# A two-layer graph network on one core: which engine turns the last 256 columns of the attention matrix, the order of the last products, the room of one tile, and four planned delays

## The chip, the core and the metric

The kernel runs on one core of a Trainium2 chip. The core has a matrix engine (TensorE, PE in the profile, with its weight loads as PEld), VectorE (DVE), ScalarE (ACT), GpSimd (POOL) and SyncE (SP), whose queue issues nearly all transfers between on-chip memory and DRAM. Each engine takes its instructions in a fixed order. The metric is the device time of one execution in microseconds. A difference of about 0.2% (some 4 us here) is what a measurement of this kernel can tell from no change.

## The reference

There are 3327 nodes with 256 features, and a sparse weighted adjacency matrix `adj`. Layer 0 makes two steps (`STEPS = 2`); each has a dense attention and a product with the normalised adjacency matrix. Layer 1 is a graph attention with four heads, masked by `adj > 0`.

```python
# layer 0, from h = relu(layernorm(x)); two steps
logits = (Xa @ W1.T @ W2.T) @ (Xa @ W3.T).T        # 3327 x 3327
probs  = softmax(logits)
A      = probs where the largest, up to a sum of 0.9, are kept, then rescaled by row
Xf, Xa = R @ Xf, A @ Xa                            # R = (adj + I) / its row sums
Z      = Z + Xf @ U1[n].T + Xa @ U2[n].T
# layer 1
e    = leaky_relu(s[:, i] + d[:, j]) where adj > 0, else -inf    # 4 heads
attn = softmax(e); out = elu(attn @ hp)            # per head, 64 columns of hp = h @ W
```

## The kernel before

Everything is fp32. The 3327 rows are padded to `NT = 26` tiles of 128 (`NP = 3328`). The program is not issued in the order of the source: each piece of work is handed to a planner (`Plan.put`) with an engine, an estimated length, a rank, the pieces it needs, the buffers it takes and gives back, and a delay `lag` after which its result is taken to be there. `Plan.order` runs through these estimates once while the program is built and writes each engine's fixed order from them. On the chip nothing of the estimates is left: an engine waits where a semaphore tells it to. A delay that is estimated too short therefore leaves the program right, but puts instructions in an order in which an engine stands and waits.

**Layer 0, one row tile of the attention.** A `Row` takes a tile `e` of 128 x 3328 (four buffers `e`, and every fifth row the room called `qq`). `logits` (L905) fills PSUM in four parts of 1024, 1024, 1024 and 255 columns; `exps` (L920) takes the exponential into `e`, with a row sum for each part, which `row_sum` adds. A search on ScalarE, GpSimd and VectorE finds a threshold for each part of a row, and `drop` (L1075, VectorE, four pieces) sets what lies below it to zero. Then the tile has to be transposed, because TensorE contracts over partitions. Of the 52 row tiles, 49 (`BLOCKED`: all 26 of step 1, 23 of step 2) go this way:

- The first 3072 columns: VectorE turns each stretch of 1024 columns in 32 x 32 blocks (`turn_blocks`, L1112), one transfer puts the stretch into DRAM (`put_blocks`, L1116, 512 KB), and four transfers bring it back with the blocks in their transposed places (`get_blocks`, L1121, 128 KB each in runs of 256 bytes). `exps` had stored the columns of these stretches with a stride of two, which makes these runs.
- The last 256 columns: TensorE turns them as two 128 x 128 products with the identity into PSUM (`turn`, L1087, tile `px`), ScalarE or VectorE copies them to `et` (L1098), and `attend` (L1105) uses them.

`attend_blocks` (L1128) multiplies the 24 returned column tiles with `rhs`; the two of `et` come in between, before the last eight. The remaining three rows of step 2 are turned on TensorE alone.

Beside it, `Full` (L1153) multiplies the adjacency matrix, loaded tile by tile (L1147), with `main` in step 1 and with `c` in step 2. These products have no hurry and stand in the order where the attention leaves TensorE free. After the attention of a row in step 1, `finish1` turns and projects it; its two results of 256 columns go to a PSUM tile `px` (two buffers for all users), ScalarE copies them to `ystage` (`stage`, L1347; two buffers), and a transfer stores them (L1358).

**Layer 1** works on four column blocks `b` of 832 nodes. For each of 26 source tiles `j`, VectorE computes the weights `e` of four heads (`exponents`, L1763, four instructions of 832 columns), TensorE multiplies them with `main` (`product`, L1779; the block is cut in two halves `c` of 416 columns) and sums them (`sums`, L1793). Two source tiles' products are followed by their two sums. Seven buffers hold `e`: four of the pool `e`, then half of the room of `c`, then both halves of the room of `rhs`. The last three may be taken once layer 0 has left the rooms. At the end of a block, `leave` copies the sums out of PSUM (L1842, L1848), and seven times TensorE turns 128 nodes (L1866), VectorE divides (L1904, L1905), ScalarE takes relu and exponential, GpSimd adds `x1` (L1918), VectorE joins (L1922) and a transfer stores. In the last block nothing follows that could hide this.

Of the kernel before, what the change touches and what calls it, by code (L numbers as in the profile page):

```python
# [587 lines left out]
def fast(  # L588
# [58 lines left out]
    with ExitStack() as l0:  # L647
# [23 lines left out]
        blocks = spill.tile([3, 4, P, 2 * P], F32, name="blocks")  # L671
# [194 lines left out]
        plan = Plan(dict(rows=1, mvs=3, pl=2, px=2, acca=1, accf=1, et=3, at=4, y=1, e2=3, mask=2, e5=1, qg=2, **BUFS))  # L866
# [4 lines left out]
        class Row:  # L871
# [3 lines left out]
                "b w t0 t1 t2 u g k2 p0 p1 p2 p3 D0 D1 D2 v z r0 s0 s1 s2 h x th tq mid dh kh fl d up h0 h1 room zs cnt "  # L875
# [38 lines left out]
            def exps(self, k):  # L914
                pl = self.pl.pop(k)
                to = self.e[:, PART * k : PART * k + pl.shape[1]]
                if k < 3 and self.i < BLOCKED[self.n]:
                    to = to.rearrange("p (g q t) -> p g t q", g=4, t=2)
                    pl = pl.rearrange("p (g t q) -> p g t q", g=4, t=2)
                S.activation(  # L920
                    to,
                    pl,
                    AF.Exp,
                    accum_out=(self.p0, self.p1, self.p2, self.p3)[k],
                )

            def row_sum(self):
                k = self.NAMES.index("p0")
                S.activation(self.sc[:, k + 4 : k + 8], self.sc[:, k : k + 4], AF.Copy, accum_out=self.s)
# [170 lines left out]
            def attend(self, g):  # L1100
# [3 lines left out]
                for j in range(4 * g, min(4 * g + 4, NT)):  # L1104
                    T.matmul(  # L1105
                        self.acc, et[:, j - 4 * g, :], rhs[self.n][:, j, :], start=(j == 0),
                        stop=j == NT - 1 and self.i >= BLOCKED[self.n],
                    )

            def turn_blocks(self, g):  # L1110
                part = self.e[:, g * PART : (g + 1) * PART].rearrange("p (g s t) -> p g t s", g=4, t=2)
                V.transpose(part, part)  # L1112

            def put_blocks(self, g):
                src = self.e[:, g * PART : (g + 1) * PART].rearrange("p (g w) -> p g w", g=4)
                nc.sync.dma_start(blocks[g].rearrange("g p w -> p g w"), src)  # L1116

            def get_blocks(self, g, o):
                part = slice(o * P // 4, (o + 1) * P // 4)
                src = blocks[g, :, :, o * P // 2 : (o + 1) * P // 2].rearrange("g (b s) w -> s (g b) w", b=4)  # L1120
                nc.sync.dma_start(self.e[part, g * PART : (g + 1) * PART].rearrange("p (c w) -> p c w", w=P // 2), src)  # L1121

            def attend_blocks(self, js, stop):
                for j in js:
# [3 lines left out]
                    T.matmul(self.acc, lhs, rhs[self.n][:, j, :], start=(j == 0), stop=stop and j == js[-1])  # L1128
# [180 lines left out]
        def finish1(row, done, rank):  # L1309
# [73 lines left out]
            y = plan.put("SP", 0.5, r + 0.3, store, needs=[a], give=["ystage"], lag=3.0)  # L1383
# [120 lines left out]
        def search(row, rank, keys, stats_of, fresh):  # L1504
# [4 lines left out]
            for g in range(2):  # L1509
# [8 lines left out]
                for k in (2 * g, 2 * g + 1):  # L1518
                    got.append(
                        plan.put("ACT", 1.15 if k < 3 else 0.5, rank - 2.5, row.exps, k, needs=[a], give=["pl"])  # L1520
# [32 lines left out]
            for o in range(4):  # L1553
                a = plan.put(
                    "DVE", 1.07 if o < 3 else 0.4, rank - 1.0, row.drop, o, needs=[a], hold=1.0 if o < 3 else 0.3,
                    lag=0.15 if o < 3 else 1.5,
# [4 lines left out]
        def attention(row, rank, total, drops, right):  # L1561
            a = None
            if row.i < BLOCKED[row.n]:
                come = []
                for g in range(3):
                    b = plan.put("DVE", 1.25, rank - 1.001, row.turn_blocks, g, needs=[drops[g]])
# [5 lines left out]
                last = plan.put("PE", 0.22, rank - 0.01, row.turn, 6, needs=[drops[3]], take=["px"])  # L1572
                last = plan.either(
                    ("ACT", 0.27, row.turned_by_s), ("DVE", 0.39, row.turned_by_v), rank - 2.6, 6, needs=[last],
                    take=["et"], give=["px"],
                )
                for j in (0, 4, 8, 12, 24, 16, 20):
                    if j == 24:
# [539 lines left out]
```

## Time and profile before

| what | value |
|---|---|
| time, median of 3 runs | 2105.58 us (2104.02 to 2105.99) |
| the profiled execution's own time | 2100.08 us |
| its span in the profile | 2098.2 us |
| granted TensorE clock, mean | 0.994 |
| DRAM read and written | 242.86 MB and 93.05 MB |

The profile's first part gives each engine's busy time; a busy TensorE includes matmuls whose ends overlap. In a timeline each line has start, length, engine, line, operation, output and inputs, shapes and count; a bracket at the end holds the idle time of that engine just before and what ended it. A table by windows has one row for a stretch, with the busy microseconds (and instruction counts) of PE, PEld, DVE, ACT and POOL, the granted TensorE clock, the busy share of the 16 DMA engines (overlapping packets can carry it over 1) and the GB/s moved.

### The profile page before, as it was taken

The page shows a single profiled execution, that of the slowest core. Times are in us where ns is not written, and L with a number is a line of the kernel's source. Part 1 is how long each engine was busy: PE and PEld are TensorE (multiplying, and loading weights), DVE is VectorE, ACT ScalarE, POOL GpSimd, SP SyncE. Part 2 cuts the span into 40 slices and gives each one's busy share as a digit, 9 for nine tenths or more (in the row PEclk, how much of TensorE's full clock was granted, in tenths as well). Part 3 has the DMA queues.
Part 4 walks back from the last instruction along what each step waited for, and adds up shares of the span by engine and source line. Part 5 has one row for each costly group of instructions (what it writes and reads, how often), then busy time and mean ns, then how long its engine had stood idle before and what let it go on. Part 6 is the DMA issues. An engine that isn't in the chain of part 4 may idle for free. (4 is left out here: it accounts for less than half of the span.)

```text
span 2098.2 us, 34334 instructions
## 1 busy us (share of the span) xinstructions
PE 2037.8 (97%) x10695; PEld 1415.2 (67%) x10695; DVE 1729.7 (82%) x4105; ACT 1300.0 (62%) x2480; POOL 990.7 (47%) x2170
## 2 busy tenths in 40 slices
PE   8999999999999989989999999999999999999997
PEld 6477777878787778767878787787877333333332
DVE  5689897778876871578998979988987999999895
ACT  5767665666556621777778776778652547465552
POOL 4476654446544630567778777777772000000001
PEclk9999999999999999999999999999999999999999
DMA  4188888678877685697787888887743544453341
GB/s 116 45 190 186 194 180 195 168 152 196 189 183 172 176 186 138 199 232 165 181 189 176 203 188 191 185 191 192 182 126 89 157 141 142 125 147 115 112 127 34
DMA packets 580513, 338.56 MB, mean 161 GB/s; under 512 B 327931, under 2 KB 533281, under 8 KB 580321
## 3 DMA queue, kind: packets, MB, share of 16 engines
q1 hardware_dynamic: 579424, 336.06, 66.4%
q8 instruction: 87, 1.43, 0.3%
q14 instruction: 106, 0.86, 0.1%
q10 hardware_dynamic: 896, 0.21, 0.0%
HBM read 242.86 MB, written 93.05 MB: 160 GB/s over the span
## 5 line engine op out<-in xcount | busy, mean ns | idle before, releaser
L959 ACT ACTIVATE junk<-e,sc 128x3327 fp8e5<-128x3327 f32 x147 | 451.0, 3068 | 31.4 <-POOL sc L996 29.8
L1128 PE MATMUL acca<-rhs,e 128*128 128x256 f32 x1872 | 426.8, 381 | 4.6 <-DMA e<-blocks 4.6
L1128 PEld LDWEIGHTS acca<-rhs,e 128*128 128x128 f32 x1872 | 364.9, 197 | 48.7 <-issue 6.0
L1153 PE MATMUL accf<-c,at 128*128 128x256 f32 x1352 | 316.5, 385 | 17.1 <-DMA at<-in_adjt_dram 8.5
L1153 PE MATMUL accf<-main,at 128*128 128x257 f32 x1352 | 313.3, 381 | 5.4 <-ACT main L1304 2.5
L1153 PEld LDWEIGHTS accf<-c,at 128*128 128x128 f32 x1352 | 252.8, 192 | 67.5 <-DMA at<-in_adjt_dram 10.2
L1153 PEld LDWEIGHTS accf<-main,at 128*128 128x128 f32 x1352 | 250.4, 190 | 54.3 <-issue 11.5
L1022 DVE MAX8 cands<-y 128x8 f32<-128x205 f32 (+1 forms) x832 | 242.9, 361 | 3.6
L1918 POOL TENSOR_TENSOR qq<-qq 128x256 f32<-128x256 f32 x4 | 3.0, 759 | 457.0 <-ACT qq L1914 457.0
L1017 DVE SCALAR_TENSOR_TENSOR y<-e,sc 128x1639 f32<-128x1639 f32 x84 | 165.1, 1965 | 62.9 <-POOL sc L1007 61.7
L920 ACT ACTIVATE e<-pl 128x1024 f32<-128x1024 f32 (+1 forms) x168 | 152.9, 920 | 75.4 <-PE pl L905 74.7
L1752 ACT ACTIVATE et<-at 128x448 bf16<-128x448 f32 (+1 forms) x204 | 112.6, 552 | 128.6 <-DVE e L1763 73.3
L1779 PE MATMUL pl<-e,main 128*64 128x416 f32 x1024 | 190.4, 517 | 0.1
L1075 DVE SCALAR_TENSOR_TENSOR e<-e,thr 128x1024 f32<-128x1024 f32 (+1 forms) x168 | 178.4, 1066 | 2.4 <-DMA at<-in_adjt_dram 0.3
L905 PE MATMUL pl<-kt,qg 64*128 64x512 f32 (+1 forms) x832 | 173.7, 536 | 0.4 <-ACT qq L920 0.4
L1112 DVE STREAM_TRANSPOSE e<-e 128x1024 f32<-128x1024 f32 x117 | 146.1, 1248 | 3.7
L1779 PEld LDWEIGHTS pl<-e,main 128*64 128x64 f32 x1024 | 70.3, 137 | 111.0 <-issue 91.5
L1763 DVE SCALAR_TENSOR_TENSOR e<-c,low,et 128x832 f32<-128x832 f32 x128 | 128.8, 1070 | 6.1 <-issue 3.2
L905 PEld LDWEIGHTS pl<-kt,qg 64*128 64x128 f32 x832 | 71.5, 186 | 83.4 <-issue 76.2
L1751 ACT ACTIVATE at<-at 128x448 f32<-128x448 f32 (+1 forms) x204 | 110.8, 543 | 25.7 <-DMA at<-in_adjt_dram 25.6
L1763 DVE SCALAR_TENSOR_TENSOR e<-qq,low,et 128x832 f32<-128x832 f32 x120 | 120.5, 1073 | 4.1 <-PE accf L1793 2.9
L959 ACT ACTIVATE junk<-qq,sc 128x3327 fp8e5<-128x3327 f32 x35 | 107.4, 3068 | 10.7 <-POOL sc L996 10.4
(550 smaller groups left out, 3540.7 us busy)
## 6 DMA issues: line engine op xcount, KB each, us to landing
at<-in_adjt_dram SPq DMA_DIRECT2D x414, 256.0 KB
blocks<-e SPq DMA_DIRECT2D x117, 512.0 KB
e<-blocks SPq DMA_DIRECT2D x468, 128.0 KB
at<-in_adjt_dram SPq DMA_DIRECT2D x102, 192.0 KB
blocks<-qq SPq DMA_DIRECT2D x30, 512.0 KB
qq<-blocks SPq DMA_DIRECT2D x120, 128.0 KB
at<-in_adjt_dram SPq DMA_DIRECT2D x52, 128.0 KB
ys<-ystage SPq DMA_DIRECT2D x26, 256.0 KB
```

Source lines behind the costliest of these rows:

```text
L905: T.matmul(pl[:, lo : lo + m], qg[self.n, self.i // 4][half, self.i % 4, :], kt[half, 512 * k : 512 * k + m], start=True, stop=True,)
L920: S.activation(to, pl, AF.Exp, accum_out=(self.p0, self.p1, self.p2, self.p3)[k],)
L959: S.activation(junk[:, :N], self.e[:, :N], fn, bias=t, scale=-1.0, accum_out=dst, saturate=False)
L1017: V.scalar_tensor_tensor(self.y[:, : hi - lo], self.e[:, lo:hi], self.up, self.e[:, lo:hi], ALU.is_lt, ALU.mult, accum_out=(self.h0, self. ...
L1022: V.max(self.cands[:, a * PIECES // 2 + k, :], self.y[:, at[k] - lo : at[k + 1] - lo])
L1075: V.scalar_tensor_tensor(piece, piece, self.thr[:, o : o + 1], piece, ALU.is_gt, ALU.mult)
L1112: V.transpose(part, part)
L1128: T.matmul(self.acc, lhs, rhs[self.n][:, j, :], start=(j == 0), stop=stop and j == js[-1])
L1153: T.matmul(self.acc[:, : self.w], self.at[j // JC][:, j % JC, :], self.src[:, j, : self.w], start=(j == 0), stop=(j == NT - 1),)
L1752: S.activation(to, src, AF.Sign)
L1763: V.scalar_tensor_tensor(held["e"][:, k, :], extra["both"][b % 2][:, k, :], low[:, j, k : k + 1], held["mask"], ALU.max, ALU.mult,)
L1779: T.matmul(q["acc"][a][k * FH : (k + 1) * FH, c, :C], main[:, j, h * FH : (h + 1) * FH], held["e"][:, h, c * C : (c + 1) * C], start=(j == 0),
```

## The change

- **Last 256 columns.** The third stretch of a blocked row is now 1280 columns. VectorE turns it in one instruction, which needs the third and fourth `drop`; it is put with one transfer of 640 KB and comes back with four of 160 KB. The two products with the identity, their copy and `attend` on `et` are gone for these rows. `exps` writes the last part with two instructions of 128 and 127 columns, each with its own sum.
- **Last products of layer 1.** In the last block, the last six source tiles are multiplied and summed for the first half of the columns, one tile after the other, then for the second half. The first half is copied out and its three turns stand between the products of the second.
- **Room of the first tile.** The tiles `j` with `j % 7 == 0`, so also `j = 0`, use half of the room of `c`; the four buffers of the pool follow.
- **Delays in the plan.** Store of `ystage`: 7.0 in place of 3.0; loads of the adjacency matrix: 4.0 in place of 3.3; after the fourth `drop`: 0.15 in place of 1.5.

In the built program TensorE has 98 products with the identity fewer (78 in place of 176 on the attention tiles); the number of products with `rhs` is the same. In the order that the planner writes, all products of `Full` in step 2 now stand ahead of the first product of layer 1; before, 26 of them stood between its first four matmuls and the rest.

```diff
@@ class Row
             def exps(self, k):
                 pl = self.pl.pop(k)
-                to = self.e[:, PART * k : PART * k + pl.shape[1]]
-                if k < 3 and self.i < BLOCKED[self.n]:
-                    to = to.rearrange("p (g q t) -> p g t q", g=4, t=2)
-                    pl = pl.rearrange("p (g t q) -> p g t q", g=4, t=2)
...
+                to = to.rearrange("p (g q t) -> p g t q", q=P, t=2)
+                if k < 3:
+                    S.activation(to, pl.rearrange("p (g t q) -> p g t q", g=4, t=2), AF.Exp, accum_out=sums[k])
+                else:
+                    S.activation(to[:, 0, 0, :], pl[:, :P], AF.Exp, accum_out=self.p3)
+                    S.activation(to[:, 0, 1, : m - P], pl[:, P:], AF.Exp, accum_out=self.p4)
...
+            def part(self, g):
+                return self.e[:, g * PART : (g + 1) * PART if g < 2 else NP]
+
             def turn_blocks(self, g):
-                part = self.e[:, g * PART : (g + 1) * PART].rearrange("p (g s t) -> p g t s", g=4, t=2)
+                part = self.part(g).rearrange("p (g s t) -> p g t s", s=P, t=2)
                 V.transpose(part, part)
@@ def finish1
-            y = plan.put("SP", 0.5, r + 0.3, store, needs=[a], give=["ystage"], lag=3.0)
+            y = plan.put("SP", 0.5, r + 0.3, store, needs=[a], give=["ystage"], lag=7.0)
@@ def search (drops)
-                    lag=0.15 if o < 3 else 1.5,
+                    lag=0.15,
@@ def attention
-                    b = plan.put("DVE", 1.25, rank - 1.001, row.turn_blocks, g, needs=[drops[g]])
+                    b = plan.put(
+                        "DVE", 1.25 if g < 2 else 1.55, rank - 1.001, row.turn_blocks, g, needs=drops[g : g + 1 + g // 2]
+                    )
...
-                last = plan.put("PE", 0.22, rank - 0.01, row.turn, 6, needs=[drops[3]], take=["px"])
-                last = plan.either(
-                    ("ACT", 0.27, row.turned_by_s), ("DVE", 0.39, row.turned_by_v), rank - 2.6, 6, needs=[last],
-                    take=["et"], give=["px"],
-                )
-                for j in (0, 4, 8, 12, 24, 16, 20):
-                    if j == 24:
-                        a = plan.put("PE", 0.864, rank, row.attend, 6, needs=[last, a], give=["et"])
-                        continue
+                for j in range(0, NT - 2, 4):
+                    js = range(j, j + 4 if j < 20 else NT)
                     a = plan.put(
-                        "PE", 1.728, rank, row.attend_blocks, range(j, j + 4), j == 20, needs=[come[j // 8], a, right],
+                        "PE", 0.432 * len(js), rank, row.attend_blocks, js, needs=[come[j // 8], a, right],
@@ def full
-                plan.put("SP", 0.4, rank, f.load, q, needs=[after], take=["at"], lag=3.3) for q in range(-(-NT // JC))
+                plan.put("SP", 0.4, rank, f.load, q, needs=[after], take=["at"], lag=4.0) for q in range(-(-NT // JC))
@@ def attend_neighbours
+            LATE = 6
...
-                                if k < 4
-                                else extra["e"][k - 4]
+                                if 0 < k < 5
+                                else extra["e"][max(k - 4, 0)]
...
+                    if b == 3 and j >= NT - LATE:
+                        for c in range(2):
+                            r = rank if c == 0 else r0 + 9.0
+                            p_ = plan.put("PE", 0.71, r, product, 0, (c,), needs=[x_, last_acc, halves[c]])
+                            p_ = plan.put("PE", 0.71, r, product, 1, (c,), needs=[x_, y_, p_])
+                            halves[c] = plan.put(
+                                "PE", 0.76, r, sums, (c,), needs=[p_, last_den], give=[mine] if c else []
+                            )
+                        continue
...
+                def leave_half(c, q=q):
+                    if c == 0:
+                        q["ot"] = scr.tile([P, 2 * W], F32, name="y").rearrange("p (k w) -> p k w", k=2)
+                        q["ot"] = [q["ot"][:, 0], q["ot"][:, 1], extra["den"]]
+                    for k in range(2):
+                        S.copy(q["ot"][k][:, c * C : (c + 1) * C], q["acc"][k][:, c, :C])
+                    S.copy(q["ot"][2][:, c * C : (c + 1) * C], q["den"][c][:, :C])
```

## The prediction

> **What bounds the kernel now.** I read the busy times first, then the table by windows, then TensorE's waits, then the timeline around the longest of them and at the end.
>
> ```profile
> PE 2037.8 (97%) x10695; PEld 1415.2 (67%) x10695; DVE 1729.7 (82%) x4105; ACT 1300.0 (62%) x2480; POOL 990.7 (47%) x2170
> ```
>
> ```profile
> 700.00:800.00 100.00, 92.07 (x416) 75.44 (x415) 72.14 (x197) 34.13 (x64) 37.87 (x83) 0.97 0.91 201
> ...
> 1100.00:1200.00 100.00, 98.28 (x466) 80.82 (x466) 91.63 (x264) 74.34 (x137) 79.94 (x173) 1.00 0.85 190
> ...
> 1700.00:1800.00 100.00, 100.00 (x735) 37.03 (x733) 98.39 (x115) 60.33 (x153) 0.00 (x0) 1.00 0.49 142
> ```
>
> TensorE is the bound nearly everywhere: 98 of 100 us in the attention, 100 in layer 1, with VectorE close behind (92 and 98). What it does not work it waits, and a share of that has names:
>
> ```profile
> PE accf L1153 <- DMA at<-in_adjt_dram: 10.5, 6, 6.2
> PE px L1087 <- ACT ystage L1347: 8.5, 3, 7.2
> PE accf L1153 <- ACT main L1164: 5.4, 5, 3.4
> PE acca L1128 <- DMA e<-blocks: 4.6, 6, 1.7
> ```
>
> ```profile
> 334.59 0.38 PE L1087 MATMUL px<-ident,e 128*128 128x128 f32 x2
> 334.81 1.90 PE L1153 MATMUL accf<-main,at 128*128 128x257 f32 x8
> ...
> 750.99 0.59 ACT L1347 COPY ystage<-px 128x512 f32<-128x512 f32 x1 [9.55 <-DMA ys<-ystage]
> 751.63 0.69 PE L1087 MATMUL px<-ident,e 128*128 128x128 f32 x2 [7.18 <-ACT ystage L1347]
> 752.11 3.25 PE L1128 MATMUL acca<-rhs,e 128*128 128x256 f32 x8
> ...
> 907.24 5.99 PE L1153 MATMUL accf<-c,at 128*128 128x256 f32 x16 [6.18 <-DMA at<-in_adjt_dram]
> ...
> 1164.49 1.97 PE L1128 MATMUL acca<-rhs,e 128*128 128x256 f32 x8 [1.72 <-DMA e<-blocks]
> ```
>
> The reader is to see three things. Two turns hold TensorE for 0.22 us (334.59 to 334.81). At 751 ScalarE waits for the store of an earlier `ystage`, keeps a tile `px`, and a turn waits for that. After such a gap the work is slow: eight matmuls take 3.25 us where they take 1.97 at 1164, sixteen take 5.99 where 3.62 is usual; the granted clock of that window is 0.97.
>
> **The change part by part.** The sum is made in the profiled execution's time, 2100.08 us; the median of the runs shown is 5.5 us above it.
>
> *The turns of 49 rows.* 98 products with the identity go: 49 x 0.22 = 10.8 us off the bounding engine. The products on `et` become products on `e` of the same 0.38 us. Hidden: the longer turn on VectorE, 1.248 x 1280/1024 = 1.56, so 49 x 0.31 = 15 us, against 20 copies of 0.42 that go; the extra exponential on ScalarE. One of 255 columns takes 0.385 and its read 0.20; the shortest ScalarE rows are 0.19, so one of 128 is near 0.29 and the pair adds 0.39, 19 us in all, against 29 copies of 0.37 that go. VectorE idles 8 us in 100 in the fullest attention window above, ScalarE 25; these cover it. Without the cover VectorE's net 7 us would lie on the path. Term -10.8.
>
> *The wait for `px`.* A blocked row took four tiles `px` and takes three; the turn that waited 7.18 us no longer exists, and a store planned at 7.0 lets the planner put ScalarE's copy later. The gap cost 7.18 and then 3.25 - 1.9 = 1.4 of slow work; two more such waits cost 1.3. What is late next is the projection of the next row, which takes the following `px`; the attention and `Full` stand between. Bounds: -9.9 (all gone) to 0 (another taker waits instead). I take -9.9, since the waiting instruction is removed.
>
> *The loads of the adjacency matrix.* At 907 the loads stand on SP's queue behind eight `get_blocks` issues that take 8.07 us from 894.11. In the new order two loads stand after each four. Gap plus slow work: 6.18 + 2.4 = 8.6. Bounds -8.6 to 0; half, -4.3, because these four-issue groups each carry more bytes.
>
> *The later third stretch.* It waits for a fourth `drop` (0.45) and 0.31 more of turning: 0.76 us. It moves 256 KB more per row, which at the 190 GB/s of the window is 1.35 us. And TensorE wants it sooner: without the two `et` products (0.87) before the last eight. Together 3.0 us of slack go in each row. From the trace's packet records, the last 256-byte packet of a third stretch ended a median of 5.8 us (step 1) and 4.2 us (step 2) before the matmul that needs it; where TensorE did stand waiting, this distance was 1.4 to 2.3, so about 1.5 of it is completion and cannot be used. Usable now 4.3 and 2.7; left 1.3 and -0.3. Each stall moves TensorE back against VectorE and gives the next rows slack, so I do not pay it 23 times. Bounds: 0, to 0.5 us in each of 49 rows, 25 us. I take 6, a little above the 4.6 that waits on `e<-blocks` cost now. Behind a waiting matmul stands everything on TensorE: the logits of later rows, `Full`, and with them ScalarE and VectorE. On SP the larger puts and gets are as many as before (147 and 588), and the loads behind a put now wait for the longer turn; the four loads ahead (`at`) cover 0.3 us.
>
> The Trainium skill speaks against this part twice. "VectorE: DVE Perf Modes", section "Rules for kernel authors", gives a 128 x 128 transpose to TensorE when PSUM may hold the result, because VectorE turns only blocks of 32 x 32. By that rule the part would be a loss: its gain of 10.8 would go and its cost of 6 would stay, a sum 10.8 higher. The page's ground is the path alone; here 0.22 us of the full engine is traded for time of engines with idle time. "DMA: Bandwidth & Descriptors", section "Specifications", wants at least 512 bytes in a run for full rate; the returns are 256. Its section "Why small descriptors are slow" has 11 cycles for 8 of data at this size; an estimate by it makes the returning half 0.68 x 11/8 = 0.93 and the slack lost 3.3 in place of 3.0, up to 0.3 x 49 = 15 us if all of it came on the path.
>
> *Start of layer 1.* The first tile now needs the room of `c`, so VectorE cannot start before the last product of `Full`. Until now it had the instructions of two source tiles done (two at 1571.7, six at 1595.5) while TensorE still worked. Two of them take 2.08 us, one `product` of eight recorded matmuls about 1.45; TensorE waits 2.1 for the first pair, then 2.0 - 1.45 = 0.6 three times: 3.9 to 4.2. Before, the same starvation cost 7.32 - 5.81 = 1.5 (at 1626). Net +2.7; bounds -1.5 to +4.2. Nothing hides it: no work of layer 0 is left in TensorE's order there.
>
> *Products by halves.*
>
> ```profile
> 2065.94 5.81 PE L1779 MATMUL pl<-e,main 128*64 128x416 f32 x32
> 2071.68 0.91 PE L1793 MATMUL acca<-e,qd 128*32 128x416 f32 x8
> ...
> 2082.46 0.88 PE L1793 MATMUL accf<-c,qd 128*32 128x416 f32 x8
> ...
> 2085.03 3.04 POOL L1918 TENSOR_TENSOR qq<-qq 128x256 f32<-128x256 f32 x4 [457.00 <-ACT qq L1914]
> ...
> 2090.02 1.60 DVE L1922 SCALAR_TENSOR_TENSOR e<-e 128x256 f32<-128x256 f32 x3
> ```
>
> A pair of matmuls starts every 0.35 us; from 2065.94 to 2071.68 there are 16 pairs, 5.59, and 0.15 remains: the price of going from products to sums. Six tiles in pairs change 6 times; by halves 24 times: 18 x 0.145 = 2.6. Three turns of 0.33, with two more breaks, move between the products: 1.6. So the last sum ends 4.2 later. From it (2083.34) to the last join (2091.62) are 8.28 now, paced by seven additions on GpSimd of 0.76 to 0.87. With four left: ScalarE's copies end 0.9 after the sums, the first addition starts 1.8 after that (as 83.22 to 85.03 now), four take 3.2, and the last join ends about 0.95 after: 6.9. Gain 1.4, net +2.8. Bounds: +0.2 if the breaks cost nothing, +4.2 if the tail keeps its length.
>
> *Sum.* -10.8 - 9.9 - 4.3 + 6 + 2.7 + 2.8 = -13.5: 2086.6 for the profiled execution, 2092 for the median.
>
> **The rivals.** *The third stretch becomes the wait (slower).* Without its 6 the sum is -19.5; it takes 19.5/49 = 0.40 us per row to break even and 0.49 to be 0.2% slower. For it: the median usable slack in step 2 goes just below zero, and the waits of step 2 (1.72 at 1164) show that the order is already tight. Against: VectorE and ScalarE idle, so a late TensorE gets ahead of nothing. If each row paid 1 us, 49 - 19.5 = +29: 2135; at 0.65, 2118, which I take as its time. *The waits only move (no change).* The gap at 751 and that at 907 come back at other places: +14.2 on the sum, 0.7 up, 2106. For it: ScalarE waits 46 us in all for stores of `ystage`; against: the taker is gone. *All waits go.* The stretch costs nothing, 907 goes whole: -13.5 - 6 - 4.3 = -24: 2082.
>
> **How the numbers follow.** The forecast's own case has 0.47 (2084 to 2101), all waits go 0.20, no change 0.15, slower 0.18. Lower end by the bounds: -10.8 - 9.9 - 8.6 + 0.2 - 1.5 = -30.6, or 2075; I set 2077. Upper end: 2112, which leaves the worse half of the slower rival out. About 0.2%, 4 us, can be told from no change: below 2101.4 lie the first two and a little of the third, 0.69; within 0.13; above 2109.8, 0.18.
>
> **What would show it.** Right: L1087 with 78 products, no gap of 7 us near 750, TensorE's waits for `e<-blocks` under 12 us, a gap of 2 us or more just ahead of the first product of layer 1, and from the last sum to the last join about 7 us. Wrong: waits for `e<-blocks` of 20 us or more in step 2, or a new wait for `px` or `ystage` of several microseconds between 700 and 920; then the turns' 10.8 us are spent again.

## The result, and the profile after

The changed kernel takes 10854.86 us (10850.77 to 10857.21, four runs); the kernel before 2104.8 in the same comparison. The ratio is 5.157, with a 95% interval of 5.148 to 5.166. The prediction had 2092 and nothing above 2112.

From the page of the changed kernel, its span, TensorE's busy tenths in 40 equal slices and one of the costliest groups:

```profile
span 10855.4 us, 68374 instructions
...
PE   9999999822222222222321333333332221106666
...
L201 DVE SCALAR_TENSOR_TENSOR scr<-e,cand 128x3327 bf16<-128x3327 f32 x1404 | 5124.5, 3684 | 35.8 <-ACT e L182 12.7
```

The number of instructions is twice that of before, TensorE is busy for one fifth of the span as before (eight slices of forty) and then hardly, and a line that did not run before, L201, takes 5.1 ms of VectorE. L201 belongs to a second program in the same kernel. The kernel ends like this, before the change as after it:

```python
        fast(tc, again, *args)
        with tc.If(tc.nc.values_load(again, min_val=0, max_val=1) > 0):
            general(tc, *args)
```

`fast` is all that the document has told of so far. It finds the threshold of a row by a search that does not succeed for every input, tests each row, and writes a verdict to `again`; `general`, slower and valid for any input, then does everything once more. One test asks about equal weights: the weights of a row are kept in falling order up to the sum of 0.9, and where two equal weights stand on both sides of the cut, `fast` can keep one and drop the other only if they lie in different parts of 1024 columns. The trace of before shows the results of all tests being gathered, in its timeline:

```profile
1837.59 0.20 DVE L2056 TENSOR_REDUCE far<-bad 128x1 f32<-128x52 f32 x1
```

In the timeline of the changed kernel the planned work ends with its last joins and stores, and the second program begins at once:

```profile
2091.58 2.13 DVE L1947 SCALAR_TENSOR_TENSOR e<-e 128x256 f32<-128x256 f32 x3
...
2093.67 0.38 ACTq L130 DMA_DIRECT2D w<-in_w1t_dram  x1
...
2094.19 0.09 DVE L194 MEMSET cut<- 128x2 f32 x2 [0.47 <-DVE e L1947]
```

So two things have to be explained: the 8.76 ms behind 2093.7, and the planned work itself. Its last join ends at 2093.7 where it ended at 2091.6 before, 2.1 us later, and the prediction's sum was -13.5. For that part, the table by windows answers to the rows shown of before:

```profile
700.00:800.00 100.00, 95.95 (x437) 79.96 (x437) 67.88 (x188) 31.37 (x51) 32.03 (x69) 1.00 0.92 199
...
1100.00:1200.00 100.00, 93.91 (x433) 75.62 (x435) 87.42 (x239) 72.40 (x132) 72.11 (x155) 1.00 0.87 187
```

TensorE is busier at 700 (96.0 us in place of 92.1) and less busy at 1100 (93.9 in place of 98.3). Its waits, up to the end of the planned work:

```profile
PE accf L1158 <- DMA at<-in_adjt_dram: 12.2, 10, 2.6
PE px L1441 <- ACT xa L1436: 6.6, 5, 3.3
PE accf L1158 <- DVE main L1172: 6.3, 6, 3.4
PE pl L1780 <- DVE c L1764: 3.5, 1, 3.5
PE acca L1133 <- DMA e<-blocks: 3.4, 4, 1.5
...
PE px L1450 <- DVE xt L1445: 3.0, 2, 1.7
```

The wait for `ystage` is gone. Longer than before are the waits at L1441 and L1450, the two small steps that turn and project a row of step 2 after its normalisation (`finish2`), and the one for L1172, the addition that frees `accf`. Before, the two small steps had other line numbers, and the first of them cost this:

```profile
PE px L1436 <- ACT xa L1431: 0.6, 1, 0.6
```

### The profile page after: what moved, and what is told of

Read it like the earlier page. It is cut to its first block, busy times and chain, and to the rows that moved or that the text cites. A ratio compares the mean times of both kernels' runs of the same rounds, so it can differ in the third digit from the quotient of the medians.

```text
span 10855.4 us, 68374 instructions
## 1 busy us (share of the span) xinstructions
PE 4889.8 (45%) x21465; PEld 3209.1 (30%) x21465; DVE 10118.9 (93%) x12193; ACT 2858.4 (26%) x4942; POOL 1048.2 (10%) x2281
## 4 chain that ended last, share of the span: by engine, by line
DVE 68%; PE 8%; issue 2%; ACT 1%; another core or an unknown queue 0%; DMA 0%; POOL 0%; SPq 0%; ACTq 0%; POOLq 0%; DVEq 0%
DVE scr L201 41%; DVE e L440 4%; DVE junk L390 3%; DVE scr L219 3%; DVE e L448 3%; PE acc L260 2%; PE pl L176 2%; DVE scr L223 2%; DVE e L215 2%; DVE e L224 2%; DVE e L444 1%; DVE mx L179 1%; DVE cand L197 1%; PE pm L285 1%; DVE cut L207 1%
## 5 line engine op out<-in xcount | busy, mean ns | idle before, releaser
L201 DVE SCALAR_TENSOR_TENSOR scr<-e,cand 128x3327 bf16<-128x3327 f32 x1404 | 5124.5, 3684 | 35.8 <-ACT e L182 12.7
L449 PE MATMUL acc<-e,hp 128*65 128x512 f32 (+1 forms) x1456 | 716.1, 639 | 348.8 <-DVE e L448 348.8
L440 DVE SCALAR_TENSOR_TENSOR e<-both,sd,e 128x512 f32<-128x512 f32 (+1 forms) x728 | 475.3, 728 | 8.8 <-ACT e L439 8.7
L439 ACT ACTIVATE e<-both,dlow 128x512 f32<-128x512 f32 (+1 forms) x728 | 443.7, 678 | 51.2 <-PE acc L449 51.2
L448 DVE SCALAR_TENSOR_TENSOR e<-adjb,e 128x512 f32<-128x512 f32 (+1 forms) x728 | 430.9, 667 | 4.0 <-ACT e L445 3.8
L390 DVE CUSTOM_DVE_ANT_0 junk<-an,db 128x3327 bf16<-128x3327 f32 (+1 forms) x104 | 370.7, 3624 | 2.0 <-ACT db L375 1.2
L219 DVE TENSOR_TENSOR_SCAN scr<-scr 128x3327 uint16<-128x3327 bf16 x52 | 368.5, 7086 | 0.0
L176 PE MATMUL pl<-kt,qt 64*128 64x512 f32 (+1 forms) x728 | 353.7, 628 | 1.2 <-ACT e L177 1.2
L260 PE MATMUL acc<-main,et 128*128 128x257 f32 x1352 | 353.7, 409 | 0.0
L260 PE MATMUL acc<-xa,et 128*128 128x257 f32 x1352 | 342.3, 399 | 3.8 <-ACT et L253 3.8
```

The costliest lines, as they stand in the source:

```text
L176: T.matmul(pl[:, :w], qt, kt[:, c : c + w], start=True, stop=True)
L201: V.scalar_tensor_tensor(junk, e[:, :N], cand[:, g : g + 1], e[:, :N], ALU.is_ge, ALU.mult, accum_out=sums[:, g : g + 1],)
L219: V.tensor_tensor_scan(rank, ties, ties, 0.0, ALU.add, ALU.max)
L260: T.matmul(acc, et[:, j - j0, :], src[:, j, :], start=(j == 0), stop=(j == NT - 1))
L390: V.tensor_tensor_reduce(junk[:p], an[:p], db[:p, k, :N], scale=1.0, scalar=-BIG, op0=ALU.add, op1=ALU.max, accum_out=top[:p, t, k : k + 1],)
L439: S.activation(e[:, k, :w], both[:, 1, k, :w], AF.Identity, bias=dlow[:, j, k : k + 1])
```

## The experiments

Two theories for the second program. *Equal weights*: the change makes the sums of the attention in another order, step 2's logits come out with other last bits, and some row has equal weights at its cut. *Wrong weights* (rival): the new turn, or the row sum split in two, is wrong somewhere. For the planned work, three: the wide third stretch is what TensorE waits for (the prediction's term, and its slower rival); the longer instructions on VectorE and ScalarE cost the gain; or the written order does, by where it puts small steps.

In the table, "idle" is the length of a window less TensorE's busy time in it; 48 to 825 us is step 1, 825 to 1489 most of step 2. Every ratio is to the kernel before on the same chip (median 2097.8 to 2099.2). "Alone" means that the second program and its branch are left out; e10 to e16 are alone as well.

| run | kernel | median us | ratio, 95% interval | idle step 1 | idle step 2 |
|---|---|---|---|---|---|
| | before | 2099 | 1 | 18.1 | 18.4 |
| e3 | before, alone | 2096.97 | 0.9984 (0.9974 to 0.9995) | 15.5 | 18.3 |
| e2 | changed, alone | 2092.77 | 0.9971 (0.9959 to 0.9984) | 9.6 | 28.6 |
| e4 | changed, old order of additions | 2095.92 | 0.9987 (0.9977 to 0.9997) | 8.5 | 28.1 |
| e6 | e4 with the old end of layer 1 | 2094.35 | 0.9977 (0.9968 to 0.9985) | 10.1 | 26.9 |
| e7 | before + wide stretch, alone | 2098.75 | 0.9996 (0.9985 to 1.0007) | 13.3 | 29.1 |
| e17 | before + store delay, alone | 2079.59 | 0.9906 (0.9890 to 0.9921) | 4.3 | 19.2 |
| e18 | before + load delay, alone | 2104.30 | 1.0023 (1.0014 to 1.0032) | 17.0 | 23.7 |
| e8 | before + both delays, alone | 2078.32 | 0.9907 (0.9892 to 0.9922) | 5.0 | 21.0 |
| e9 | before + both delays, whole | 2079.55 | 0.9919 (0.9905 to 0.9932) | 5.0 | 22.3 |
| e12 | e8, turns of step 2 four times | 2085.76 | 0.9935 (0.9919 to 0.9951) | 5.0 | 13.9 |
| e10 | e8 + wide stretch in step 1 | 2082.06 | 0.9929 (0.9916 to 0.9942) | 7.2 | 19.9 |
| e11 | e8 + wide stretch | 2088.74 | 0.9959 (0.9947 to 0.9972) | 8.5 | 28.2 |
| e15 | e11, VectorE's turn short in step 2 | 2086.46 | 0.9928 (0.9916 to 0.9941) | 9.5 | 26.0 |
| e16 | e11, one exponential | 2090.45 | 0.9957 (0.9942 to 0.9973) | 8.7 | 27.9 |
| e13 | e11, stretch planned 2 us later | 2079.18 | 0.9897 (0.9883 to 0.9912) | 10.0 | 22.0 |
| e14 | e8, stretch planned 2 us later | 2081.65 | 0.9916 (0.9903 to 0.9929) | 4.9 | 18.4 |

### Why the second program ran: e1, e2, e4, e5

**e1: which test fails, and in which row.** In place of the second program stand 21 branches, each of which writes a mark of its own length when its flag is set.

```diff
-        with tc.If(tc.nc.values_load(again, min_val=0, max_val=1) > 0):
-            general(tc, *args)
...
+        for k in range(MARKS):
+            with tc.If(nc.values_load(again[:1, k + 1 : k + 2], min_val=0, max_val=128) > 0):
+                nc.vector.memset(again[32:33, : k + 1], 0)
```

> The changed kernel; the second, slow program behind its verdict is left out, and in its place up to 21 marks are written, one for each test that failed: the step, the test, how many rows, which row. If equal weights at the cut are the cause (theory: the sums of the attention are made in another order, the logits of step 2 differ in their last bit, and one or a few rows then have equal weights where the cut falls): a mark for step 2 and none for step 1, of the five tests only that of the equal weights, one to three rows, and a time near 2110 us with the marks. If the new turn of the last 1280 columns delivers wrong weights (rival): marks for other tests or for both steps, and many rows. If a wait or a transfer were the cause, no test would fail.

Measured: 2112.4 us, and seven marks in the timeline:

```profile
2093.92 0.06 DVE L2168 MEMSET again<- 1x2 int32 x1 [0.79 <-DVEq L2167]
2097.10 0.06 DVE L2168 MEMSET again<- 1x6 int32 x1 [3.12 <-DVEq L2167]
2099.90 0.07 DVE L2168 MEMSET again<- 1x10 int32 x1 [2.74 <-DVEq L2167]
2101.29 0.07 DVE L2168 MEMSET again<- 1x12 int32 x1 [1.33 <-DVEq L2167]
2101.98 0.07 DVE L2168 MEMSET again<- 1x13 int32 x1 [0.62 <-DVE again L2168]
2105.49 0.07 DVE L2168 MEMSET again<- 1x18 int32 x1 [3.44 <-DVEq L2167]
2106.88 0.07 DVE L2168 MEMSET again<- 1x20 int32 x1 [1.32 <-DVEq L2167]
```

The length of a mark (1 to 21) is its meaning. 2: a row failed in step 2; 1, for step 1, is missing. 6: the test of equal weights; 3, 4, 5 and 7, the other four, are missing, and so are 8 and 9, for more than one and more than two rows. 10, 12 and 13 are the bits 1, 4 and 8 of the tile, the 13th; 18 and 20 the bits 8 and 32 of the row in it, the 40th. One row out of 6654 (3327 in each step) fails, in step 2, because of equal weights at its cut.

**e2 and e3: the planned work by itself.** The two lines of the branch are left out of the changed kernel (e2) and of the kernel before (e3).

> The changed kernel without the second program and without the branch to it. Equal weights: the output is as near to the reference as that of the kernel before, and the time is that of the planned work, which in the trace of the changed kernel ends 2.1 us later than before: 2107 us, between 2103 and 2110. The prediction's sum for the planned work said 2092. Wrong weights: the same time, and an output far from the reference.

> The kernel before without the second program and without the branch to it: what the branch costs when it is not taken. Both theories: the same planned work, 2105 us less 0 to 4.

Measured: 2092.77 and 2096.97. The branch costs 2.2 us where it is not taken. The planned work is 4.2 us shorter by these medians, 0.13% by the ratios, whose intervals overlap, where the prediction had 13.5. That 2092.77 stands beside the forecast of 2092 is luck: the forecast counted from a median of 2105.58, and here the kernel before takes 2096.97 without its branch.

**e4: the changed kernel with the old order of additions.** Column tiles 24 and 25 come ahead of 16, as they do in the kernel before; the flag that ends the sum moves with them, and nothing else differs.

```diff
...
-                    js = range(j, j + 4 if j < 20 else NT)
+                    js = list(range(j, j + 4)) if j < 16 else [24, 25, 16, 17] if j == 16 else [18, 19, 20, 21, 22, 23]
```

> The whole changed kernel with its second program; only the order of the last ten products with rhs is another: column tiles 24 and 25 ahead of 16 and 17 to 23 in place of behind them. The same work, the same transfers. Equal weights: the last bits come out differently once more, and with luck no row has equal weights at its cut: 2107 us, between 2100 and 2112. Wrong weights: the second program runs as before, 10855 us.

Measured: 2095.92 us. The page says how much is executed:

```profile
span 2091.4 us, 34205 instructions
```

The second program is still in the kernel and does not run. The expectation calls this order a new one, which only luck would spare; it is that of the kernel before. The turn, the transfers and the split row sum are those of the changed kernel, so none of them is at fault.

**e5: the kernel before with the changed kernel's order of additions alone.**

```diff
...
-                for j in (0, 4, 8, 12, 24, 16, 20):
+                for j in (0, 4, 8, 12, 16, 20, 24):
...
```

> The whole kernel before, second program included, with one change: the two products on the tiles that TensorE turned (column tiles 24 and 25) stand behind those of 16 to 23 in place of ahead of them, which is the order of additions of the changed kernel. Nothing is turned, moved or delayed otherwise. Equal weights: the logits of step 2 come out with other last bits, a row has equal weights at its cut, and the second program, which took 8761 us, runs: 10855 to 10870 us. If the new turn or the split row sum is needed for the failure: 2097 to 2106 us.

Measured: 10850.26 us. The page:

```profile
span 10848.5 us, 68500 instructions
...
L201 DVE SCALAR_TENSOR_TENSOR scr<-e,cand 128x3327 bf16<-128x3327 f32 x1404 | 5124.4, 3684 | 32.1 <-ACT e L182 9.3
```

Moving two products of 26 behind eight others makes the kernel before five times slower. That is the cause, shown from both sides: with the second program in place, each of two orders of these additions ran in both kernels. With the old one (before, e9; e4, e6) it never runs, with the new one (changed; e5) it does. Which test failed was read out in the changed kernel alone (e1); that it is the same one in e5 is inferred. How often an order of additions meets such a row no run shows.

### Where the planned work's gain went: e6 to e18

**e6: the end of layer 1.** e4 with the old last block: no products by halves, `leave` and the turns as before.

> The whole changed kernel with the other order of the last ten products with rhs, and with the end of layer 1 as before (no products by halves). From the products of the last six source tiles to the last join the halves took 46.0 us and the old end 43.0. If nothing hides that: 3 us less than the same kernel with halves, 2093 us where the kernel before has 2099 (2090 to 2095). If the halves save behind the last join what they cost ahead of it: 2096.

Measured: 2094.35, 1.6 us less than e4, which the intervals do not tell from nothing. In the traces the stretch of 46.0 us is 43.0 long, as expected (it is counted from the products of the last eight tiles; the expectation names six).

**e7, e8: the wide stretch and the delays apart.** e7 takes the wide stretch alone from the change, e8 the two numbers 7.0 and 4.0 alone. The third delay, 0.15 after the fourth `drop`, goes with the wide stretch; the change has no fourth.

> The kernel before with the wide third stretch alone (the turn of 1280 columns on VectorE, its transfers, the two exponentials, the short delay after the fourth drop); old room, old end, old delays; the second program and the branch to it are left out. The prediction's terms: 10.8 us of products with the identity go, 6 come back as waits for the stretch: 2097 less 4.8, 2092. If waits for other engines take the place of the work in step 2 (new theory): TensorE's busy time is 10 us less, its idle time in step 2 some 8 us more, and the time is 2094 to 2098.

> The kernel before with the two planned delays alone (7.0 for the store of the staged results, 4.0 for the loads of the adjacency matrix); the second program and the branch to it are left out. If the delay alone removes the wait of 7.2 us for the staged results and shortens that of 6.2 for the loads: idle time in step 1 falls by 8 us, and the time is 2085 to 2090. If waits only move: 2094 to 2099, with the idle time of TensorE up to layer 1 the same within 3 us as the 40 to 42 of the kernel before.

Measured: 2098.75 and 2078.32. The wide stretch alone gives +1.8 us on e3, which the intervals do not tell from nothing, with 10.8 us more idle time in step 2; the delays alone give -18.7, more than the prediction had for them and far more than the change as a whole.

**e17, e18: the delays apart.**

```diff
-            y = plan.put("SP", 0.5, r + 0.3, store, needs=[a], give=["ystage"], lag=3.0)
+            y = plan.put("SP", 0.5, r + 0.3, store, needs=[a], give=["ystage"], lag=7.0)
```

```diff
-                plan.put("SP", 0.4, rank, f.load, q, needs=[after], take=["at"], lag=3.3) for q in range(-(-NT // JC))
+                plan.put("SP", 0.4, rank, f.load, q, needs=[after], take=["at"], lag=4.0) for q in range(-(-NT // JC))
```

> The kernel before with the delay of the store of the staged results alone (7.0 in place of 3.0); the second program and the branch are left out. The prediction's term for this wait: 2097 less 9.9, 2087 (2084 to 2090), with TensorE's idle time in step 1 down from 15.5 to about 7 us. If the delay only moves the wait: 2094 to 2099.

> The kernel before with the delay of the loads of the adjacency matrix alone (4.0 in place of 3.3); the second program and the branch are left out. The prediction's term: 2097 less 4.3, 2093 (2089 to 2097). If the two delays only add and the store's gives 9.9: 2097 less 8.8, 2088.

Measured: 2079.59 and 2104.30. The store's delay gives all of it, -17.4 us; the loads' delay alone costs 7.3, and on top of the store's it costs nothing (e8 against e17: -1.3). TensorE's largest wait in e17:

```profile
PE accf L1153 <- DMA at<-in_adjt_dram: 10.2, 10, 1.9
```

and, of e18, up to layer 1:

```profile
PE px L1087 <- ACT ystage L1347: 7.6, 2, 7.1
```

The last number is the longest single wait. With the store's delay no wait for `ystage` is left, and that for the loads, 5.4 us at its longest in e3, is 1.9: the store's delay took the second gap away as well, though the loads' waits still add up to 10.2 (11.1 in e3). The loads' delay left both gaps and the sum of the loads' waits (10.9); at 746 its clock is granted by half for 10.2 us.

**e9: the whole kernel before with the two delays.**

> The whole kernel before, second program included, with the two planned delays alone (7.0 and 4.0). No sum is made in another order, so no row can come to fail that did not: the second program does not run. The time of the same kernel without the branch was 2078.3 us and the branch costs about 2.2 (2099.2 less 2097.0): 2080.5, between 2077 and 2087. If the gain hung on leaving out the branch: 2095 or more.

Measured: 2079.55 us, ratio 0.9919 (0.9905 to 0.9932). With its second program in place and with the old order of additions this is the fastest whole kernel of the study: it beats both.

**e10, e11, e12: the wide stretch on top of the delays.** e10 has it in step 1 only, e11 in both steps, e12 keeps the narrow stretch and repeats its turns in step 2.

```diff
-                    T.transpose(pt[:, k, :], self.e[:, j * P : (j + 1) * P], ident)
+                    for _ in range(4 if self.n == 1 and m == 2 and self.i < BLOCKED[1] else 1):
+                        T.transpose(pt[:, k, :], self.e[:, j * P : (j + 1) * P], ident)
...
```

> The kernel before with the two delays and the wide third stretch in step 1 only (26 rows); step 2 turns its last 256 columns on TensorE as before; the second program and the branch are left out. If the gain of the turn is lost in step 2 alone: 26 x 0.22 = 5.7 us less than the 2078.3 with the delays alone, 2072.6 (2069 to 2076). If the wide stretch costs as much as it saves in step 1 too: 2077 to 2083.

> The kernel before with the two delays and the wide third stretch in both steps; old room, old end; the second program and the branch are left out. If the two edits only add: 2078.3 plus the 1.8 that the turn alone cost, 2080 (2077 to 2083). If the wide stretch spoils what the delays gain in step 2: 2092.8 of the changed kernel less the 3 of the halves, 2090 (2087 to 2093); the same number says that the room of the first tile costs nothing.

> The kernel before with the two delays; in the 23 blocked rows of step 2 each of the two products with the identity is done four times, in the same order of all instructions: 138 products more, 138 x 0.11 = 15.2 us of TensorE; the second program and the branch are left out. If TensorE's work sets the pace of step 2: 2078.3 + 15 = 2093 (2090 to 2096), and the idle time of TensorE in step 2 stays near 21 us. If something else sets it, idle time takes up the added work: 2078 to 2086, with idle time in step 2 down to 8 to 14.

Measured: 2082.06, 2088.74, 2085.76. In step 1 the wide stretch does not pay (+3.7 on e8, with some 4 us of uncertainty, where 5.7 less was to be had). In both steps it costs 10.4: the edits do not add, and what is lost shows mostly in step 2 (idle 28.2 in place of 21.0, and 8.5 in place of 5.0 in step 1). In e12 TensorE has 15.2 us more to do in the same order and the time rises by 7.4, while idle time in step 2 falls from 21.0 to 13.9: about half of what TensorE is given there reaches the end (by the intervals, between a tenth and two thirds).

**e13 to e16: instructions or order.** All four are variants without the second program. e15 and e16 keep the written order of e11 and shorten one suspect each; e13 changes the order of e11, and e14 that of e8, by two numbers that are used only while the program is built.

```diff
-                    b = plan.put("SP", 0.5, rank - 1.0, row.put_blocks, g, needs=[b], lag=6.0)
+                    b = plan.put("SP", 0.5, rank - 1.0, row.put_blocks, g, needs=[b], lag=6.0 if g < 2 else 7.0)
...
-                        [plan.put("SP", 0.6, rank - 1.0, row.get_blocks, g, o, needs=[b], lag=5.5) for o in range(4)]
+                        [plan.put("SP", 0.6, rank - 1.0, row.get_blocks, g, o, needs=[b], lag=5.5 if g < 2 else 6.5) for o in range(4)]
```

> As with the two delays and the wide stretch in both steps (2088.7 us), every instruction in the same order; in step 2 VectorE's third turn covers 1024 columns and not 1280 (1.25 us and not 1.52), and the last 256 columns stay unturned. If VectorE's longer instruction costs the time: 23 x 0.27 = 6 us less, 2083 (2080 to 2085). If not: 2086 to 2091.

> As with the two delays and the wide stretch in both steps (2088.7 us), every other instruction in the same order; the last 255 columns take one exponential and one read of its sum in place of two and two (0.4 us of ScalarE less in each of 49 rows), so these columns stand in another order and meet the wrong rows of rhs. If ScalarE's second exponential delays the steps that TensorE waits for: 5 us less or more, 2080 to 2084. If not: 2086 to 2091.

> As with the two delays and the wide third stretch in both steps (2088.7 us), but the planner is told that the third stretch lands 2 us later (its put 7.0 in place of 6.0, its returns 6.5 in place of 5.5). Nothing of the work changes, only the written order. If the landing of the third stretch is what TensorE waits for: 2083 or less. If the place of small steps in the order decides (steps of step 2's normalisation behind long VectorE instructions), any other order gives another time: 2080 to 2096, and the count of GpSimd's additions over 1.2 us there (24 of 48) changes with it. If the longer instructions themselves cost it: 2087 to 2091.

> As with the two delays alone (2078.3 us, narrow stretch), with the third stretch planned 2 us later in the same way. Only the written order changes. If the delays' gain does not hang on one order: 2076 to 2082. If it was the luck of one order: 2084 to 2096.

Measured: 2086.46 (e15), 2090.45 (e16), 2079.18 (e13), 2081.65 (e14). ScalarE's second exponential is not it. What VectorE's longer turn costs e15 leaves open: 2.3 us of the 10.4 by the medians, but 0.31% or 6.5 us by the ratios, whose intervals do not meet, where 6 were asked. It does not settle the loss either way, since e13 has the same long turns. The order that the planner writes is worth 9.6: the same work in another order is as fast as with the narrow stretch. The table by windows, step 2, of e11 and then of e13:

```profile
825.00:1489.00 664.00, 635.79 (x2914) 507.68 (x2913) 557.80 (x1527) 490.52 (x873) 484.21 (x1051) 0.99 0.85 194
825.00:1489.00 664.00, 642.01 (x2955) 514.62 (x2951) 565.85 (x1553) 495.45 (x886) 496.92 (x1066) 0.99 0.88 198
```

In step 2 e13's TensorE is busy 6.2 us longer in the same window, with the same work to do: it is further on. (The planner also chooses the engine of some copies: of the copies to `xt` at L1445, e11 has eight on VectorE and e13 four.) What TensorE waits for in e11, and hardly in e13, is not the stretch. It is the chain of `finish2`; the waits of e11 (two lines) and of e13:

```profile
PE px L1441 <- ACT xa L1436: 6.6, 5, 3.3
PE px L1450 <- DVE xt L1445: 3.2, 3, 1.7
...
PE px L1441 <- ACT xa L1436: 1.6, 1, 1.6
```

One such wait in e11's timeline:

```profile
1041.28 1.95 DVE L1019 SCALAR_TENSOR_TENSOR y<-qq,sc 128x1688 f32<-128x1688 f32 x1
1041.45 1.85 POOL L693 TENSOR_SCALAR mv<-mv 128x1 f32<-128x1 f32 x1 [1.75 <-DVE mv L688]
...
1044.49 0.59 ACT L1436 ACTIVATE xa<-ystage,mv 128x256 f32<-128x256 f32 x1
...
1045.13 0.44 PE L1441 MATMUL px<-ident,xa 128*128 128x128 f32 x2 [1.05 <-ACT xa L1436]
```

GpSimd adds one number per partition (L693) in 1.85 us while VectorE runs a long instruction of the search. In e9 the same line is mostly short:

```profile
925.36 0.22 POOL L693 TENSOR_SCALAR mv<-mv 128x1 f32<-128x1 f32 x1 [1.12 <-DVE mv L688]
```

In e11 all 24 additions over 1.2 us run beside this instruction (L1019); of the 24 others, two do for a part. Between 830 and 1600 us the addition takes over 1.2 us in 24 of some 49 recorded cases in the orders of e2, e4, e6, e11, e15 and e16, and in 13 to 16 in those of e3, e8, e9, e12, e13, e14 and e17; idle time in step 2 is 26 to 29 us in the former and 14 to 22 in the latter. e18 lies between, with 19 and 23.7. The traces of the changed kernel (24 and 30.1) and of before (12 and 18.4) fit. That the two numbers go together is seen in the traces; no experiment was made on the addition itself. e7 has idle time of 29 with only 13 long additions: there TensorE waits 21.1 us for the loads (11.1 in e3), so an order can lose the time in another way.

The Trainium skill has this in "SBUF — State Buffer", section "SBUF: two separate sides": VectorE and GpSimd share a pair of ports, an instruction of VectorE with two inputs from SBUF that starts first locks it against GpSimd's reads for its whole length, and GpSimd waits. The rows agree: 0.22 us without and 1.85 beside 1.95 of VectorE.

## Why the prediction was wrong, point by point

**The step that failed** is in "The turns of 49 rows": "The products on `et` become products on `e` of the same 0.38 us." Their length was right, and their place in the sum was not looked at: they moved from between tiles 15 and 16 to behind tile 23. The sum in fp32 then has other last bits (not read out, but e4 and e5 differ from their kernels in this order alone), one row of step 2 gets equal weights at its cut (e1), and a branch that the profile of before never takes is taken. No term, no rival and no bound of the prediction had a value in it: a changed last bit stood at nothing, without a reason. Both signs were to be had before: the branch in the source behind `fast`, and rows of `bad`, `far` and `verdict` in the trace.

**The signs.** All five signs of being right that the prediction named are in the trace: the 78 products, no gap near 750, waits for `e<-blocks` of 3.4 us, a gap of 3.5 ahead of layer 1, and 6.0 us from the last sum to the last join. None of them was a sign of the time.

**The turns, -10.8.** L1089 stands in the groups by line with 78 products, as said:

```profile
L1089 PE MATMUL px<-ident,e 128*128 128x128 f32 x78 | 11.0, 273 | 0.4 <-DVE e L1077 0.4
```

The work went, the time did not follow. The cover on ScalarE held (e16); for VectorE it is open (e15). What was wrong is "off the bounding engine": in step 2 about half of a change in TensorE's work reaches the end (e12), and the order that the planner then wrote lost the rest (e11 to e13).

**The wait for `px`, -9.9.** Right in kind: the wait is gone and idle time in step 1 falls from 15.5 (e3) and 18.1 (before) to between 6.7 and 9.6 in the changed kernel (its own trace, e1, e2). As a term it was mis-sized: the delay of the store alone is worth 17.4 (e17), with the gap at 907 in it. The prediction had put this gain down to the removed taker as well; with the taker still there, the delay alone does it. With the taker gone and the old delay (e7) the wait for `ystage` is gone too, but other waits leave idle time in step 1 at 13.3.

**The loads, -4.3.** The gap at 907 is gone, but the wait as a whole did not shrink: it is 12.2 us in the changed kernel in place of 10.5, shorter each time and more often. The loads' own delay did not take the gap away (e18, e17). Alone it costs 7.3, and not in this wait, which stays at 10.9 (11.1 in e3).

**The later third stretch, +6.** The place was wrong. Waits for the stretch are 3.4 us in place of 4.6, under the 12 that were named. The loss of 10 us in step 2 is real and stands elsewhere, at L1441, L1450 and `accf`; of the prediction's two signs of failure neither came. It is closest to the rival *the waits only move*, which let the two gaps come back at other places without saying where.

**Start of layer 1, +2.7.** The wait for the room is there, in the timeline:

```profile
1614.97 5.83 PE L1780 MATMUL pl<-c,main 128*64 128x416 f32 x15 [3.50 <-DVE c L1764]
```

It costs nothing net that these runs can tell: from the last row's logits to the ninth source tile e2 takes 164.2 us and e11, with the old room, 164.1.

**Products by halves, +2.8.** Measured +3.0 in the traces. The last sum comes 5.3 us later where 4.2 was worked out (from the products of the last eight tiles 40.0 in place of 34.7), and from it to the last join are 6.0 us in place of 8.28, where 6.9 was worked out.

**The sum.** -13.5 was foretold for the planned work; e4 against the kernel before gives 0.13%, 2.7 us. By the medians of the runs the sum has other terms: the delays -18.7 (e8 on e3), the wide stretch on top of them +10.4 (e11), the new room and the halves together +4.0 (e2 on e11), in all -4.2 (e2 on e3). Of the 10.4, e13 gives 9.6 back by the order alone. Why the wide stretch gains nothing even then is known in part. In step 1 its traces on top of the delays (e10, e11, e13) have 7.2 to 10.0 us of idle time where the narrow ones (e8, e9, e12, e14) have 4.9 to 5.0. In all three wide traces TensorE then waits for the loads near 320, 729 and 761 us, 3.6 to 3.9 in all; in e8, e9 and e14 no such wait is listed in step 1. So most of the 5.7 us that step 1 was to save goes to waits for the loads, against which the prediction counted the four tiles ahead as cover. Why they come late was not tried. In step 2 the cause stays open: e13 waits 13.0 us for the loads there, e8 9.6 and e14 6.2. Against e14, run beside it, e13 is 2.5 us faster, which the intervals do not tell from nothing. No order was found in which the wide stretch clearly pays.

## What to carry to other kernels

Before any duration is priced, ask whether the change alters a value, be it in the last bit, and whether something in the kernel branches on values: a changed order of additions is a change of values, and a fallback has a price of its own. Where a planner writes the order, a change of work is also a new draw of the order; the draw is worth as much here (10 us) as the work, so a gain has to be shown in more than one order before it is believed or given up. A single mis-estimated delay, the store's 3.0, was worth more than all that the change did by hand.

## What the runs showed of the hardware

- One column added on GpSimd took 0.22 us alone (e9) and up to 1.95 beside a two-input instruction of VectorE (e11); through a chain of small steps it reached TensorE.
- The granted clock fell to one half in stretches of 3.4, 6.8 or 10.2 us, most of them at a gap of TensorE. In e11, behind the gap of 2.67 us that ends at 1265.1, by windows:

```profile
1267.40:1270.80 3.40, 3.40 (x9) 2.70 (x8) 3.33 (x8) 3.39 (x6) 2.69 (x4) 0.50 1.37 173
```

0.50 is the clock. Half of each stretch is lost: up to 2060 us 8.5 in all in the kernel before, 11.9 in the changed one, none in the profiled run of e9. "TensorE: Matmul & The Clock Gate" in the Trainium skill, section "What's actually happening", gives such a window the same length.

- Two traces of one written order (e8 and e9) reach the ninth source tile of layer 1 at 1643.5 and 1634.3 us; a single trace does not settle differences of a few microseconds here.
